# Mixer output contracted over 128 + 64 channels, the last 64 of two tiles side by side on halves of the rows

## The chip, the cores and the metric

The kernel runs on one core of one Trainium2 chip. The metric is the time of one execution on the device in microseconds; a smaller number is better. The core has a matrix engine (TensorE, PE in the profile, with its weight loads as PEld), a vector engine (DVE), a scalar engine (ACT), GpSimd (POOL), and SyncE (SP), which here only starts DMA transfers. Each engine works through its own instructions in order, and they wait for each other at semaphores.

## The reference

An input of 32 images, 56 x 56 pixels with 96 channels, goes through two layers. Layer 0 is attention in shifted windows of 7 x 7 and a quantized feed-forward part. Layer 1 is a mixer with a recurrence along the width, and another feed-forward part of the same kind. Each part is added to its input, after a layer normalization. What matters here is the mixer:

```python
x = _layernorm(inputs, ln_gamma, ln_beta)
x_proj = jnp.einsum('bhwc,ce->bhwe', x, W_expand)
gate = jax.nn.sigmoid(jnp.einsum('bhwc,ce->bhwe', x, W_gate))
ssm_out = _ssm_scan(x_proj, A, B, C, D)
gated = gate * ssm_out
return jnp.einsum('bhwe,ec->bhwc', gated, W_out)
```

Here `c` runs over 96 channels and `e` over 192. The last line, which contracts the 192 gated channels to 96, is what the change concerns.

## The kernel before

A block is 14 image rows (784 pixels), held as 7 tiles `g` of 112 pixels by 96 channels in `xb`. There are 128 blocks, four to an image. All work on a block is cut into about a hundred named steps, such as `q` (queries and keys), `sc` (scores), `av` (values), `hf0` to `yf` (feed-forward of layer 0), `pu0` to `pu3` (the mixer's two projections), `gt0`, `gt1`, `so` (its output) and `hg0` to `yg` (feed-forward of layer 1). Steps that begin with `h` or `y` and end in `f` or `g` belong to the layer with that letter: `hf` and `yf` to layer 0, `hg` and `yg` to layer 1.

The order of the work is written out by hand in tables: `PIPELINED`, with `FILL` for the first 7 rounds and `DRAIN` for the last ones. In round `t` an entry `name:lag` runs step `name` for block `t - lag`. So each engine has a fixed order, in which some 11 blocks overlap. The six scan steps `SC0` to `SC5` and their gates `GA0` to `GA5` run once for a whole image, in one round of four.

All PSUM tiles come from one pool of four buffers of two banks each (`banks`), so a step on PE also waits until an earlier step's result has been read out of the buffer that it gets.

In the mixer, the scan leaves its gated result in `gts`, with pixels of a row pair on the partitions (two rows of 56 in 64 each) and 192 channels along the free side. To contract over channels, PE first transposes: `gt0` does tiles 0 to 3 and `gt1` tiles 4 to 6, each tile as two halves of 96 channels, L884. ACT copies the results to `gT` (steps `eg0`, `eg1`, L894), whose partitions 96 to 127 are zero. Step `so` then multiplies each tile in two matmuls that add up in PSUM, one for each half of 96 channels, L905: 14 matmuls over 128 rows of the array, of which 96 hold data. Step `as` (L513, shared with `ad`) adds the result to `xb` on DVE.

Float32 matmuls show as two records each in the profile; transposes show as one. A matmul has a tile of the array: all 128 x 128, or a part of it such as 64 x 64 (the scans and `av`), 128 x 64 (`q`, `v`), 128 x 32 (`k`) or 32 x 64 (`sc`); parts that don't overlap can work at the same time. The profile writes rows and columns as `64*64`.

Of the kernel before, what the change touches and what calls it, by code (L numbers as in the profile page):

```python
# [8 lines left out]
F32 = mybir.dt.float32  # L9
# [4 lines left out]
ALU = mybir.AluOpType  # L14
# [9 lines left out]
C = 96  # L24
HW = 56
# [5 lines left out]
E = 2 * C  # L31
EH = E // 2
RS = 64
UNIT = 16
NS = 16
TP = 2 * HW
G = 7
NBLK = 4
# [15 lines left out]


PIPELINED = (
    "rf2:4 r0:5 hf0:4 GA2:9 cf1:4 SC0:9 zg:11 GA0:9 ex2:3 ex0:3 pu1:5 SC5:9 xf0:4 pu0:5 th1:5 av:3 "
    "cf2:4 GA5:9 bg:11 uc1:5 pu2:5 th0:5 sa:1 rc:3 ta:2 rf0:4 uc0:5 uc2:5 th2:5 cf0:4 pa:1 ea:2 pg:10 "
    "tro:3 yf:4 eo:3 kg:11 gt0:9 zf:4 pr:3 ng:10 pu3:5 bf:4 eg0:9 kf:4 ad:3 th3:5 sf:3 uc3:5 pf:3 k:2 "
    "tg:10 se:4 ek:2 pe:4 SC1:8 gt1:9 eg:10 eg1:9 q:2 GA1:8 eq:2 hg0:10 nf:3 xg0:10 hg1:10 rg0:10 "  # L60
    "SC3:8 xg1:10 ne:4 so:9 SC4:8 as:9 hg2:10 GA3:8 ST:11 v:2 tf:3 cg0:10 GA4:8 xg2:10 sc:2 ev:2 te:4 "
    "ef:3 rg1:10 hf1:3 xe:4 rg2:10 cg2:10 cg1:10 st1:2 st2:2 xf1:3 ex1:2 hf2:3 xf2:3 SC2:8 st0:2 "
    "yg:10 sg:9 na:1 LD:0 rf1:3 "
)

FILL_ROUNDS = 7
FILL = (
    "gt0:9 hf0:4 r0:5 SC1:8 gt1:9 pu0:5 xf0:4 pg:10 ex2:3 hg1:10 SC2:8 ex0:3 pu1:5 eg:10 GA0:9 rf2:4 "
    "cf1:4 pu2:5 xg1:10 th1:5 uc0:5 th2:5 SC5:9 rg1:10 ng:10 uc1:5 th0:5 ST:11 cg0:10 rg0:10 uc2:5 "
    "cf2:4 sa:1 rf0:4 av:3 cf0:4 eg0:9 so:9 SC0:9 rc:3 kg:11 sg:9 GA2:9 zg:11 GA5:9 GA3:8 yf:4 zf:4 "  # L70
    "tro:3 as:9 cg2:10 bf:4 kf:4 se:4 pa:1 ta:2 xg2:10 eo:3 GA1:8 rg2:10 ea:2 pe:4 pr:3 q:2 k:2 ad:3 "
    "ek:2 bg:11 LD:0 yg:10 tg:10 pu3:5 uc3:5 cg1:10 sf:3 GA4:8 eq:2 th3:5 v:2 ne:4 ev:2 te:4 pf:3 "
    "sc:2 xe:4 nf:3 tf:3 st1:2 ef:3 st0:2 st2:2 ex1:2 hf1:3 eg1:9 xf1:3 hg2:10 xg0:10 na:1 SC4:8 "
    "hg0:10 hf2:3 xf2:3 SC3:8 rf1:3 "
)
DRAIN_FROM = 2
DRAIN = (
    "hf0:4 rf2:4 cf2:4 r0:5 SC5:9 xf0:4 LD:0 pu3:5 v:2 zg:11 pu2:5 uc3:5 eq:2 bg:11 st0:2 rf0:4 pg:10 "
    "pu1:5 ex0:3 GA2:9 sa:1 cf1:4 th3:5 q:2 cf0:4 GA5:9 ng:10 th2:5 kg:11 ex2:3 uc2:5 yf:4 uc1:5 na:1 "
    "SC0:9 GA0:9 st1:2 sc:2 th1:5 av:3 gt0:9 rc:3 zf:4 st2:2 bf:4 ea:2 tro:3 eo:3 eg0:9 ek:2 tg:10 "  # L80
    "pr:3 pu0:5 eg:10 ad:3 gt1:9 hg2:10 sf:3 uc0:5 kf:4 se:4 eg1:9 pf:3 xg2:10 th0:5 SC4:8 nf:3 "
    "hg0:10 tf:3 hg1:10 ta:2 rg2:10 xg1:10 pe:4 cg2:10 SC3:8 rg1:10 ef:3 pa:1 ne:4 xg0:10 GA4:8 "
    "cg1:10 GA3:8 rg0:10 so:9 cg0:10 as:9 ev:2 hf1:3 hf2:3 SC2:8 ST:11 ex1:2 te:4 xf2:3 yg:10 xf1:3 "
    "SC1:8 xe:4 GA1:8 sg:9 rf1:3 k:2 "
)

IN_TURN = (
# [10 lines left out]
def kernel(  # L98
# [27 lines left out]
    nc = tc.nc  # L126
# [3 lines left out]
    const = ctx.enter_context(tc.tile_pool(name="const", bufs=1))  # L130
# [8 lines left out]
    def banks(name):  # L139

        return psum.tile([128, 2, 512], F32, tag="ps", name=name)
# [15 lines left out]
    xtiles = {}  # L157
# [3 lines left out]
    def zeros(size, name):  # L161
        t = const.tile([128, size], F32, name=name)
        nc.gpsimd.memset(t, 0.0)
        return t

    wqkv = zeros(3 * C, "wqkv")
    ident = zeros(128, "ident")
# [2 lines left out]
    wo = zeros(C, "wo")  # L170

    weg = zeros(2 * E, "weg")
    wso = zeros(2 * C, "wso").rearrange("p (h c) -> p h c", h=2)
    mask = zeros(W2, "mask")
    low = zeros(W2, "low")
# [22 lines left out]
    gts = [const.tile([128, NRP, E], F32, name=f"gt_{n}") for n in range(2)]  # L198
# [55 lines left out]
    n = 1  # L254
# [18 lines left out]
    pt = banks("tapsT")  # L273
# [47 lines left out]
    for par in range(2):  # L321
        half = mask[par * 64 : par * 64 + 64, :]
# [3 lines left out]
        half = low[par * 64 : par * 64 + 64, :]  # L326
# [15 lines left out]
    pt = banks("bias1")  # L342
# [25 lines left out]
    for n, (w1, b1_, w2, b2_) in enumerate(((f0_w1, f0_b1, f0_w2, f0_b2), (f1_w1, f1_b1, f1_w2, f1_b2))):  # L368
        w1s = stage(128, 3 * C).rearrange("p (h c) -> p h c", h=3)
        nc.scalar.dma_start(w1s, w1.rearrange("(h p) c -> p h c", p=128))  # L370
        pt = banks(f"w1t_{n}")
# [7 lines left out]
        pt = banks(f"w2t_{n}")  # L379
# [21 lines left out]
    nc.scalar.dma_start(bet, beta[:, None])  # L401
    nc.scalar.dma_start(weg[0:C, 0:E], w_gate)
    nc.scalar.dma_start(weg[0:C, E : 2 * E], w_expand)
    nc.scalar.dma_start(wso[0:C], ssm_w_out.rearrange("(h p) c -> p h c", p=C))


    xws, vs, gTs, xqs = [], [], [], []
    for n in range(2):
        xw = const.tile([128, NTOK + OVER], F32, name=f"xw_{n}")
        nc.vector.memset(xw[C:, :], 1.0)  # L410
        nc.vector.memset(xw[0:C, NTOK:], 0.0)
        xws.append(xw)
        gT = const.tile([128, 4 - n, 2, TP], F32, name=f"gT_{n}")
        nc.vector.memset(gT[C:], 0.0)
        gTs.append(gT)
        xq = const.tile([128, NTOK], F8, name=f"xq_{n}")
        nc.vector.memset(xq[C:], 0.0)
        xqs.append(xq)
        v = const.tile([128, NPAIR * NH, HD + 1], F32, name=f"v_{n}")
        nc.vector.memset(v[:, :, HD:], 1.0)  # L420
        vs.append(v)
    ot = const.tile([128, G, 2 * NPAIR, WS], F32, name="ot")
    nc.vector.memset(ot[C:], 1.0)

# [12 lines left out]
    held = {}  # L437

    def steps(*names):


        def enter(f):
            if len(names) == 1:
                step[names[0]] = f
            else:
                for k, n in enumerate(names):
                    step[n] = lambda i, k=k: f(i, k)
            return f

        return enter  # L450
# [50 lines left out]
    def out_banks(name):  # L501

        po = banks(name)
        return [
            (g0, g1, po[0:TP, k, 0 : (g1 - g0) * C].rearrange("p (g c) -> p g c", c=C))
            for k, (g0, g1) in enumerate(((0, 4), (4, G)))
        ]

    def add_out(n):
        def add(i):  # L510
            xb = xtiles[i]
            for g0, g1, po in held.pop((n, i)):
                nc.vector.tensor_tensor(xb[:, g0:g1, :], po, xb[:, g0:g1, :], ALU.add)  # L513

        return add

    @steps("LD")
    def _(i):
        xb = xpool.tile([TP, G, C], F32, tag="xb", name=f"xb_{i}")
        for dst, src in block_dmas(i, x, xb):  # L520
            nc.sync.dma_start(dst, src)
        xtiles[i] = xb
# [190 lines left out]

    @steps("pr")
    def _(i):
        held["pr", i] = out_banks(f"pr_{i}")
        for g0, g1, po in held["pr", i]:
            for g in range(g0, g1):
                nc.tensor.matmul(po[:, g - g0, :], ot[:, g].rearrange("c w b -> c (w b)"), wo, start=True, stop=True)  # L719

# [154 lines left out]
    halves = ((0, 4), (4, G))  # L875

    @steps("gt0", "gt1")
    def _(i, k):
        g0, g1 = halves[k]
        pt = banks(f"gt_{i}_{k}")  # L880
        for g in range(g0, g1):
            for eh in range(2):
                s = (g - g0) * 2 + eh
                nc.tensor.transpose(  # L884
                    pt[0:C, s // 4, (s % 4) * 128 : (s % 4 + 1) * 128],
                    gts[i // NBLK % 2][:, (i % NBLK) * G + g, eh * EH : (eh + 1) * EH],
                    ident,
                )
        held["gt", i, k] = pt

    @steps("eg0", "eg1")
    def _(i, k):
        n = 4 * (halves[k][1] - halves[k][0])
        nc.scalar.copy(  # L894
            gTs[k][0:C].rearrange("c g h (r w) -> c (g h r) w", w=HW)[:, 0:n],
            held.pop(("gt", i, k))[0:C].rearrange("c b (s w) -> c (b s) w", w=RS)[:, 0:n, 0:HW],
        )

    @steps("so")
    def _(i):  # L900
        held["so", i] = out_banks(f"so_{i}")
        for gT, (g0, g1, po) in zip(gTs, held["so", i]):
            for g in range(g0, g1):
                for eh in range(2):
                    nc.tensor.matmul(  # L905
                        po[:, g - g0, :], gT[:, g - g0, eh, :], wso[:, eh, :], start=(eh == 0), stop=(eh == 1)
                    )

    step["as"] = add_out("so")
    feed_forward("g", 1)  # L910
# [88 lines left out]
```

## Time and profile before

| | |
|---|---|
| time, median of 3 runs | 3842.33 us (3831.57 to 3846.85) |
| the profiled execution's own time | 3844.57 us |
| its span, first to last instruction | 3842.8 us |
| mean granted TensorE clock | 0.988 |
| `so`, L905: 3584 matmul records | 377.5 us busy, 263 ns each |
| `gt`, L884: 1792 matmul records | 243.1 us busy, 276 ns each |
| copies of `gt`, L894: 256 on ACT | 209.4 us busy, 818 ns each |
| PE busy from 1000 to 2000 us | 987.13 us |

The profile has one line for each group of instructions: source line, engine, operation, result and operands, for a matmul the tile of the array, the shape, then how many. Busy time is the time in which at least one of them ran. Matmuls overlap each other in the pipeline, so the duration of one (263 ns for `so`) is more than what each adds. A timeline row merges instructions that follow each other with the same line and names: start, length, engine, line, and how many. The distance between the starts of two rows that follow each other is what the first one costs on a full engine.

### The profile page before, as it was taken

How to read it: one execution, taken by the hardware profiler on the slowest of the kernel's cores; microseconds unless marked ns; L12 is line 12 of the kernel's file. 1: busy time of each engine (PE TensorE's matmuls, PEld its weight loads, DVE VectorE, ACT ScalarE, POOL GpSimd, SP SyncE). 2: the span in 40 equal slices, each digit the busy share in tenths (PEclk: the TensorE clock that was granted, in tenths of full speed). 3: DMA queues.
4: the chain of work that ended last, by engine and by line, in shares of the span. 5: the costliest groups of instructions: out<-in, count | busy, mean ns of one | idle time of the engine just before them, and what ended most of it. 6: DMA issues, size and time to landing. Idle time of an engine off the chain costs nothing.

```text
span 3842.8 us, 178057 instructions
## 1 busy us (share of the span) xinstructions
PE 3695.3 (96%) x78628; PEld 3124.7 (81%) x78628; DVE 3247.2 (84%) x9420; ACT 2329.9 (61%) x4611; POOL 1452.0 (38%) x1176
## 2 busy tenths in 40 slices
PE   4899999999999999999999999999999999999996
PEld 3788888888888888888888888888888888888875
DVE  6788888988888888888888888888888888888875
ACT  2666666666666666566666666665566666656662
POOL 2333334443333443333443333443333433333432
PEclk8999999999999999999999999999999999999997
DMA  6001001101001111000101100101100101100100
GB/s 136 14 12 25 22 22 25 25 23 27 22 22 24 26 25 25 22 22 23 27 22 25 25 22 22 28 22 25 25 22 22 28 22 23 27 22 22 25 15 21
DMA packets 226267, 99.34 MB, mean 26 GB/s; under 512 B 218396, under 2 KB 225150, under 8 KB 225262
## 3 DMA queue, kind: packets, MB, share of 16 engines
q1 hardware_dynamic: 222522, 86.81, 10.0%
q8 instruction: 620, 10.16, 1.1%
q10 hardware_dynamic: 2964, 1.05, 0.1%
q14 instruction: 161, 1.32, 0.1%
HBM read 44.45 MB, written 43.35 MB: 23 GB/s over the span
## 4 chain that ended last, share of the span: by engine, by line
PE 91%; DVE 6%; issue 2%; ACT 1%; POOL 0%; DMA 0%; SPq 0%; DVEq 0%; ACTq 0%; POOLq 0%
PE pu L827 13%; PE scan L851 10%; PE so L905 9%; PE qk L547 8%; PE av L671 5%; PE gt L884 5%; PE pv L566 5%; PE pr L719 5%; PE pu L828 4%; PE s L589 4%; DVE pT L620 4%; PE ph_g L739 4%; PE py_g L773 4%; PE py_f L773 4%; PE tr_o L700 3%; PE ph_f L739 3%
## 5 line engine op out<-in xcount | busy, mean ns | idle before, releaser
L827 PE MATMUL pu<-weg,xs 128*128 128x288 f32 x1792 | 618.6, 427 | 2.0 <-issue 1.7
L751 ACT CAST h_g<-ph_g 128x784 f16<-128x784 f32 x384 | 300.5, 820 | 332.6 <-issue 326.0
L481 DVE TENSOR_SCALAR xn_g<-xb,st_g,rs_g 112x96 fp8e5<-112x96 f32 x896 | 365.0, 476 | 95.1 <-POOL rs_g L471 94.4
L851 PEld LDWEIGHTS scan<-u,toep 64*64 64x64 f32 x24576 | 387.8, 135 | 62.8 <-issue 42.4
L851 PE MATMUL scan<-u,toep 64*64 64x28 f32 x24576 | 413.9, 221 | 17.4 <-issue 16.4
L828 PEld LDWEIGHTS pu<-weg,xs 128*128 128x128 f32 x1792 | 339.8, 190 | 98.1 <-issue 3.5
L840 ACT COPY u<-pu 128x384 f32<-128x384 f32 (+1 forms) x512 | 229.1, 448 | 291.4 <-PE pu L828 235.3
L763 POOL CAST hq_g<-h_g 128x784 fp8e5<-128x784 f16 x128 | 122.1, 954 | 730.4 <-DVE h_g L757 461.2
L471 POOL TENSOR_TENSOR rs_a<-rs_a,neg_half 112x7 f32<-112x7 f32 x128 | 190.7, 1490 | 502.7 <-DVE rs_a L465 502.7
L905 PEld LDWEIGHTS so<-wso,gT 128*112 128x112 f32 x3584 | 372.5, 179 | 9.8 <-issue 0.9
L905 PE MATMUL so<-wso,gT 128*112 128x96 f32 x3584 | 377.5, 263 | 0.2 <-ACT h_g L751 0.2
L835 ACT ACTIVATE gt<-pu 128x384 f32<-128x384 f32 (+1 forms) x512 | 237.7, 464 | 205.9 <-PE pu L828 205.9
L866 DVE SCALAR_TENSOR_TENSOR gt<-gt,scan 128x448 f32<-128x448 f32 x384 | 220.6, 617 | 144.5 <-PE scan L851 144.4
L828 PE MATMUL pu<-weg,xs 128*128 128x96 f32 x1792 | 321.2, 261 | 3.4 <-issue 3.3
L547 PE MATMUL qk<-xw,wqkv 128*32 128x196 f32 (+1 forms) x3072 | 310.5, 394 | 4.8 <-issue 2.5
L751 ACT CAST h_f<-ph_f 128x784 f16<-128x784 f32 x384 | 308.8, 806 | 3.0 <-issue 2.8
L795 POOL TENSOR_TENSOR xb<-xb,y_f 112x672 f32<-112x672 f32 x128 | 187.3, 1463 | 293.3 <-DVE y_f L791 293.3
L827 PEld LDWEIGHTS pu<-weg,xs 128*128 128x128 f32 x1792 | 276.0, 191 | 18.7 <-issue 3.0
L620 DVE SCALAR_TENSOR_TENSOR pT<-s,bias 128x392 f32<-128x392 f32 (+1 forms) x512 | 213.7, 459 | 68.7 <-PE s L589 64.3
L739 PEld LDWEIGHTS <-w1q 128*128 128x128 fp8e5 x1536 | 123.7, 100 | 173.7 <-issue 81.3
L894 ACT COPY gT<-gt 96x896 f32<-96x896 f32 (+1 forms) x256 | 209.4, 818 | 76.4 <-PE gt L884 73.5
L481 DVE TENSOR_SCALAR xn_f<-xb,st_f,rs_f 112x96 fp8e5<-112x96 f32 x896 | 226.2, 326 | 33.4 <-POOL rs_f L471 33.4
(147 smaller groups left out, 8608.2 us busy)
## 6 DMA issues: line engine op xcount, KB each, us to landing
xb<-in_x_dram SPq DMA_DIRECT2D x224, 126.0 KB
out_dram<-xb SPq DMA_DIRECT2D x224, 126.0 KB
taps_d<-u SPq DMA_DIRECT2D x1, 4704.0 KB
xb<-in_x_dram SPq DMA_DIRECT2D x224, 13.1 KB
xb<-in_x_dram SPq DMA_DIRECT2D x224, 7.9 KB
out_dram<-xb SPq DMA_DIRECT2D x224, 13.1 KB
out_dram<-xb SPq DMA_DIRECT2D x224, 7.9 KB
xb<-in_x_dram SPq DMA_DIRECT2D x32, 72.0 KB
```

Of the source, the lines that this page charges most:

```text
L481: nc.vector.tensor_scalar(xn[:, g, :], xb[:, g, :], mean[:, col], rs[:, col], op0=ALU.subtract, op1=ALU.mult, **saturate)
L547: nc.tensor.matmul(pq[j * rows : (j + 1) * rows, m, 0:size], wqkv[:, m * C + h0 * HD : m * C + h1 * HD], xws[i % 2][:, j * size : (j + 1) ...
L620: nc.vector.scalar_tensor_tensor(view(dst), src, QSCALE, view(bt), op0=ALU.mult, op1=ALU.add)
L739: nc.tensor.matmul(ph[:, half, 0:HALF], w1q[:, hc * 128 : (hc + 1) * 128], xqs[layer][:, half * HALF : (half + 1) * HALF], start=True, sto ...
L751: nc.scalar.copy(h16.rearrange("p (h t) -> p h t", h=2), held.pop(("ph", n, i, hc))[:, :, 0:HALF])
L773: nc.tensor.matmul(po[:, g - g0, :], hq[hc][:, g * TP : (g + 1) * TP], w2q[:, hc, :], start=(hc == 0), stop=(hc == 2),)
L827: nc.tensor.matmul(pu[:, g, 0 : E + EH], rows[:, 0:128], weg[:, 0 : E + EH], start=True, stop=True)
L828: nc.tensor.matmul(pu[:, g, E + EH : 2 * E], rows[:, RS:], weg[:, E + EH :], start=True, stop=True)
L835: nc.scalar.activation(gt[:, rp : rp + n, :], held["pu", i, j][:, 0:n, 0:E], AF.Tanh, scale=0.5)
L840: nc.scalar.copy(u[:, rp : rp + n, :], held["pu", i, j][:, 0:n, E : 2 * E])
L851: nc.tensor.matmul(py[o0 : o0 + RS, eh, e * NRP : (e + 1) * NRP], toep[p * RS : (p + 1) * RS, ch * HW : ch * HW + RS], u[p * RS : (p + 1) ...
L905: nc.tensor.matmul(po[:, g - g0, :], gT[:, g - g0, eh, :], wso[:, eh, :], start=(eh == 0), stop=(eh == 1))
```

## The change

The 192 channels are contracted as 128 + 64, not as 96 + 96. The first 128 of each tile take a matmul on all rows of the array. The last 64 of an even tile lie on partitions 0 to 63 of the new buffer `gTb`, those of an odd tile on partitions 64 to 127, and their matmuls use only that half of the rows, against a copy of the same 64 rows of the weights in each half of `wso`. Even tiles go to one PSUM bank, odd tiles to the other. That makes 7 matmuls on the full array and 7 on halves of it, where there were 14 on the full array.

The transposes follow: one of 128 channels for each tile to the first bank; in the second bank, one of channels 64 to 191 for each odd tile, which leaves the last 64 on the upper partitions, and then one of the last 64 channels of each even tile, written over the lower ones. In `gt1` the last tile stands in for the odd tile that is missing. It is 15 transposes in a block, where there were 14. ACT makes four copies of them in place of two. All three tables of the order are new.

```diff
 PIPELINED = (
-    "rf2:4 r0:5 hf0:4 GA2:9 cf1:4 SC0:9 zg:11 GA0:9 ex2:3 ex0:3 pu1:5 SC5:9 xf0:4 pu0:5 th1:5 av:3 "
-    "cf2:4 GA5:9 bg:11 uc1:5 pu2:5 th0:5 sa:1 rc:3 ta:2 rf0:4 uc0:5 uc2:5 th2:5 cf0:4 pa:1 ea:2 pg:10 "
-    "tro:3 yf:4 eo:3 kg:11 gt0:9 zf:4 pr:3 ng:10 pu3:5 bf:4 eg0:9 kf:4 ad:3 th3:5 sf:3 uc3:5 pf:3 k:2 "
-    "tg:10 se:4 ek:2 pe:4 SC1:8 gt1:9 eg:10 eg1:9 q:2 GA1:8 eq:2 hg0:10 nf:3 xg0:10 hg1:10 rg0:10 "
-    "SC3:8 xg1:10 ne:4 so:9 SC4:8 as:9 hg2:10 GA3:8 ST:11 v:2 tf:3 cg0:10 GA4:8 xg2:10 sc:2 ev:2 te:4 "
-    "ef:3 rg1:10 hf1:3 xe:4 rg2:10 cg2:10 cg1:10 st1:2 st2:2 xf1:3 ex1:2 hf2:3 xf2:3 SC2:8 st0:2 "
-    "yg:10 sg:9 na:1 LD:0 rf1:3 "
+    "q:2 SC4:8 pf:3 rg2:10 xg1:10 k:2 nf:3 GA3:8 GA4:8 rg1:10 eq:2 pe:4 hg0:10 ne:4 v:2 SC2:8 cg1:10 "
+    "cg2:10 xg0:10 ek:2 ev:2 tf:3 rg0:10 ef:3 so:9 cg0:10 GA2:8 te:4 sc:2 as:9 xe:4 st1:2 st2:2 ST:11 "
+    "r0:4 hf2:3 st0:2 xf2:3 ex1:2 ex2:2 yg:10 zg:10 hf1:3 ex0:2 xf1:3 sg:9 SC0:8 pg:9 rf2:3 bg:10 "
+    "GA0:8 pu0:4 th0:4 hf0:3 rf1:3 SC5:8 LD:0 uc0:4 cf1:3 pu1:4 ng:9 GA5:8 av:2 xf0:3 rc:2 pa:1 rf0:3 "
+    "uc1:4 th1:4 gt0:8 eg0:8 tg:9 cf0:3 pu2:4 tro:2 pu3:4 kg:10 cf2:3 eg:9 yf:3 uc2:4 th2:4 sa:0 eo:2 "
+    "uc3:4 pr:2 zf:3 na:1 bf:3 th3:4 SC1:7 ad:2 ta:1 GA1:7 gt1:8 hg2:9 ea:1 sf:2 kf:3 eg1:8 hg1:9 "
+    "SC3:7 xg2:9 se:3 "
 )
...
-    nc.scalar.dma_start(wso[0:C], ssm_w_out.rearrange("(h p) c -> p h c", p=C))
+    nc.scalar.dma_start(wso[:, 0], ssm_w_out[0:128])
+    for p0 in (0, 64):
+        nc.scalar.dma_start(wso[p0 : p0 + 64, 1], ssm_w_out[128:E])
...
-        gT = const.tile([128, 4 - n, 2, TP], F32, name=f"gT_{n}")
-        nc.vector.memset(gT[C:], 0.0)
-        gTs.append(gT)
...
+    gTa = const.tile([128, G, TP], F32, name="gTa")
+    gTb = const.tile([128, (G + 1) // 2, TP], F32, name="gTb")
...
-            for g0, g1, po in held.pop((n, i)):
-                nc.vector.tensor_tensor(xb[:, g0:g1, :], po, xb[:, g0:g1, :], ALU.add)
+            for part, po in held.pop((n, i)):
+                xb = xtiles[i][:, part, :]
+                nc.vector.tensor_tensor(xb, po, xb, ALU.add)
...
         for g in range(g0, g1):
-            for eh in range(2):
-                s = (g - g0) * 2 + eh
+            nc.tensor.transpose(pt[:, 0, (g - g0) * 128 : (g - g0 + 1) * 128], gt[:, g, 0:128], ident)
+
+
+        for half in (1, 0):
+            for m in range(2):
+                g = min(g0 + 2 * m + half, G - 1)
                 nc.tensor.transpose(
-                    pt[0:C, s // 4, (s % 4) * 128 : (s % 4 + 1) * 128],
-                    gts[i // NBLK % 2][:, (i % NBLK) * G + g, eh * EH : (eh + 1) * EH],
-                    ident,
+                    pt[0 : 64 + 64 * half, 1, m * 128 : (m + 1) * 128], gt[:, g, 128 - 64 * half : E], ident
                 )
...
-        n = 4 * (halves[k][1] - halves[k][0])
-        nc.scalar.copy(
-            gTs[k][0:C].rearrange("c g h (r w) -> c (g h r) w", w=HW)[:, 0:n],
-            held.pop(("gt", i, k))[0:C].rearrange("c b (s w) -> c (b s) w", w=RS)[:, 0:n, 0:HW],
-        )
+        g0, g1 = halves[k]
+        pt = held.pop(("gt", i, k)).rearrange("c b (s w) -> c b s w", w=RS)[:, :, :, 0:HW]
+        for b, dst in ((0, gTa[:, g0:g1]), (1, gTb[:, 2 * k : 2 * k + 2])):
+            dst = dst.rearrange("c g (r w) -> c (g r) w", w=HW)
+            nc.scalar.copy(dst, pt[:, b, 0 : dst.shape[1]])
...
-        held["so", i] = out_banks(f"so_{i}")
-        for gT, (g0, g1, po) in zip(gTs, held["so", i]):
-            for g in range(g0, g1):
-                for eh in range(2):
-                    nc.tensor.matmul(
-                        po[:, g - g0, :], gT[:, g - g0, eh, :], wso[:, eh, :], start=(eh == 0), stop=(eh == 1)
-                    )
+        po = banks(f"so_{i}")[0:TP]
+        dst = lambda g: po[:, g % 2, g // 2 * C : (g // 2 + 1) * C]
+
+        for g in range(G):
+            nc.tensor.matmul(dst(g), gTa[:, g, :], wso[:, 0, :], start=(g < 2), stop=False)
+
+        for g in range(G):
+            half = slice(g % 2 * 64, g % 2 * 64 + 64)
+            nc.tensor.matmul(dst(g), gTb[half, g // 2, :], wso[half, 1, :], start=False, stop=(g >= G - 2))
+        held["so", i] = []
+        for b in range(2):
+            n = (G + 1 - b) // 2
+            held["so", i].append((slice(b, G, 2), po[:, b, 0 : n * C].rearrange("p (g c) -> p g c", c=C)))
```

`FILL` and `DRAIN` are replaced in the same way. On PE the new `PIPELINED` gives this order in a round, with the scans where a group has them: `q SC4 k hg0 v SC2 tf so te sc hf2 yg hf1 SC0 pu0 hf0 SC5 pu1 av gt0 tg pu2 tro pu3 yf pr SC1 ta gt1 hg2 hg1 SC3`. Before, it was `hf0 SC0 pu1 SC5 pu0 av pu2 ta tro yf gt0 pr pu3 k tg SC1 gt1 q hg0 hg1 SC3 so SC4 hg2 v tf sc te hf1 hf2 SC2 yg`.

## The prediction

> **What bounds the kernel now.** I read the page first, then the chain of waits, the waits of PE, the sums by stretch, and last the timeline of PE, which carries the argument.
>
> ```profile
> PE 3695.3 (96%) x78628; PEld 3124.7 (81%) x78628; DVE 3247.2 (84%) x9420; ACT 2329.9 (61%) x4611; POOL 1452.0 (38%) x1176
> ...
> PE 91%; DVE 6%; issue 2%; ACT 1%; POOL 0%; DMA 0%; SPq 0%; DVEq 0%; ACTq 0%; POOLq 0%
> ```
>
> On the page PE is busy 96% and is 91% of the chain. Next one round without scans, 25.3 us, and one with the six scan steps of a group, 39.6 us (columns: stretch, its length, busy PE, PEld, DVE, ACT, POOL, clock, DMA):
>
> ```profile
> 2066.30:2091.60 25.30, 25.11 (x425) 21.14 (x423) 23.48 (x72) 17.94 (x36) 11.23 (x9) 1.00 0.11 26
> ...
> 2116.90:2156.50 39.60, 39.23 (x1076) 33.32 (x1077) 34.11 (x98) 23.03 (x45) 12.68 (x11) 1.00 0.08 19
> ```
>
> Four rounds take 115.5 us, 32 times over. DVE works 23.5 of 25.3 us, so it is close behind. PE's largest wait from 300 to 3600 us (total, times, longest):
>
> ```profile
> PE ph_f L739 <- DVE pT L620: 21.3, 113, 0.2
> ```
>
> A busy PE isn't a useful PE: what counts is from one step's start to the next one's.
>
> ```profile
> 2021.33 0.54 PE L494 MATMUL tr_g<-ident,xn_g 112*96 112x112 fp8e5 x7
> 2021.80 2.07 PE L851 MATMUL scan<-u,toep 64*64 64x28 f32 x128
> 2023.80 0.86 PE L884 MATMUL gt<-ident,gt 128*96 128x128 f32 x6
> 2024.59 1.54 PE L547 MATMUL qk<-xw,wqkv 128*64 128x392 f32 x8
> ...
> 2028.83 2.99 PE L905 MATMUL so<-wso,gT 128*112 128x96 f32 x28
> 2031.75 0.44 PE L851 MATMUL scan<-u,toep 64*64 64x28 f32 x16
> ```
>
> ```profile
> 2056.84 1.04 PE L884 MATMUL gt<-ident,gt 128*96 128x128 f32 x8
> 2057.71 1.52 PE L719 MATMUL pr<-wo,ot 128*112 128x96 f32 x14
> ...
> 2060.68 0.55 PE L494 MATMUL tr_g<-ident,xn_g 112*96 112x112 fp8e5 x7
> 2061.06 0.82 PE L884 MATMUL gt<-ident,gt 128*96 128x128 f32 x6
> 2061.81 1.54 PE L547 MATMUL qk<-xw,wqkv 128*64 128x392 f32 x8
> 2063.28 0.84 PE L739 MATMUL ph_g<-xq,w1q 128*128 128x392 fp8e5 x4
> 2063.96 2.90 PE L905 MATMUL so<-wso,gT 128*112 128x96 f32 x28
> 2066.69 0.50 PE L739 MATMUL ph_g<-xq,w1q 128*128 128x392 fp8e5 x2
> 2067.12 1.54 PE L566 MATMUL pv<-wqkv,xw 128*64 128x96 f32 x32
> 2068.59 0.54 PE L494 MATMUL tr_f<-ident,xn_f 112*96 112x112 fp8e5 x7
> ```
>
> Between full-array steps `so` takes 2066.69 - 2063.96 = 2.73 us, 28 records (two to a float32 matmul) of 98 ns. Eight transposes take 0.87 us, 109 ns each. But `so` between two scans, which run on 64x64 tiles, takes 2.92. `tr_g` takes 0.38 before `gt` and 0.47 before a scan. The six transposes take 0.75 after `tr_g` and 0.79 after a scan, and both before `qk` on 128x64 tiles, where six of 109 ns make 0.65. So leaving a tile shape costs 0.094 us each time, and arriving 0.04 (`gt`) to 0.09 (`so`, whose first weights are then not loaded ahead). Small tiles pay for themselves by running side by side: `pv` does 32 records in 1.47 us; by the records' own starts a pair takes 0.083, and four of a scan 0.058.
>
> **What the Trainium skill says.** "TensorEngine Tiling (Array Packing)", Key Properties: changing the tiling mode, not only the tile, drains TensorE. The trace agrees: the 0.094 us above. The same page, Overview, gives up to 2x for a side of 64 or less; `pv` agrees for column halves, and so do the scans, whose four tiles share rows and columns. Its Restrictions say that column tiling excludes transpose mode for FP32 input; no transpose before is on such a tile, so the trace doesn't show it. "TensorE: Matmul & The Clock Gate", LDWEIGHTS: load time goes with columns, columns / 1.2 ns, whatever the rows; 112 columns are 93 ns, and `so` runs at 98.
>
> **The change part by part,** for a round, on PE. Tile shapes and neighbours are from the changed program's instruction order.
>
> `so`. Seven 128-row matmuls: 14 records, 1.36 us. Drain to 64x128 tiles: 0.094. Seven 64-row ones alternate between two row halves and two banks, four to three. If a pair costs what one does, by the load, that is 8 slots of 98 ns: 0.78, not 1.37. Arriving and leaving this shape: `pv` pays 1.47 - 16 x 0.083 = 0.15, its first load 64 columns; for 112 I take 0.185 (bounds 0.10 and 0.25). The next step, `te`, arrives anew: 0.04. Sum 2.46 against 2.73: -0.27.
>
> `gt0`. Six transposes of 128 columns; `pu` L828 with 128-column loads runs at 112 ns, so 0.67. Drain 0.094, two 64-column transposes 0.22, arriving and leaving 0.125 (0.09 to 0.16), next step 0.037. Sum 1.15 against 0.88: +0.27. The two narrow ones may not be single-pass on that tile: from nothing to 0.22 more here, and in `gt1` again. I take nothing: they are still issued as transposes.
>
> `gt1`. Five wide, two narrow: 0.56 + 0.094 + 0.22 + 0.125 + 0.006 before `hg2`. Sum 1.00 against 0.66 without its old drain to `q`: +0.35.
>
> Other visits to small tiles, by the new table. Before, `av`, `k`, `q`, `v` and `sc` each stand alone between full steps: 0.465 leaving, 0.197 arriving. After, `q` and `k` adjoin and the steps behind have cheaper arrivals: 0.458 together. -0.20.
>
> Scans, per four rounds. Before, six lone visits: 0.889. After, `SC4` stands between `q` and `k`, `SC2` behind `v`, `SC3` before `q`; three are lone: 0.469. -0.42.
>
> Four rounds: 4 x (-0.27 + 0.27 + 0.35 - 0.20) - 0.42 = +0.2 us, about +5 us in 32. In the whole program changes of shape go from 1640 to 2196: the halved products earn 0.59 x 128 = 75 us, and drains and transposes spend it.
>
> So waits decide. PE's four rounds without any wait sum to 112.35 us before, from its steps' usual times and these drains; the trace has 115.5: 3.2 us of waits, 100 in all. Half of it is one wait: the second `ph_f` starts 0.69 us after the first, where 0.17 is a run of them, because its bank waits until DVE has read the scores (`pT` L620). In the new order `hf2` takes the bank that `so` left, and `hf1` that of `hf2`; the score banks go to `pu0` and `hf0`, 1.76 and 3.18 us after `sc`, when DVE is done 1.7 after. That stall goes. Next late is DVE: I laid its new order along PE's by hand with the durations of before; `xn_a` is done 0.4 us before `ta` wants it, `xn_f` 0.6 before `tf`, and `GA5` 0.9 before `gt0`. With a scan round, `SC0` and `SC5` wait for no bank, where they waited 0.4 and 0.2. I take 1.5 us left per four rounds (bounds 0.8, the irregular rest, and 4): -1.7 x 32 = -54.
>
> At nothing: `gT` evicted by four copies, not two (163 ns + 0.87 per column from the 192 and 384 column `th`: 1.72 us against 1.63, ACT being 39% idle; uncovered it is 0.1 us per round), and `so`, behind which all of PE would queue, finds `gTb` written some 4 us before in that layout; the added output in strided slices of the same size; two more loads of `wso` on ACT's queue, first used near 210 us; two memsets fewer; `turn_toep` a round earlier, its table landed by 78 us and DVE there at 95 before, some 86 after, while PE still idles. Stores wait on SP for POOL's last add, then loads for stores: some 8 us, against about 24 from `kg:10` to the next round's `sa:0`, and 1176 POOL instructions keep their sizes. Ramp and drain I hold at +-10.
>
> Sum: span 3842.8 + 5 - 54 = 3794. The profiled execution was 3844.6, the median 3842.3, so this reads 3794 on the median's scale too; a little ramp for the finer steps, +4, gives 3798.
>
> **Rivals.** (1) The waits only move: DVE at 93% binds where I left it 0.4 us. For it: the slack is less than one `xn_a`. Against: the old order shows no such wait. 3842 + 5 = 3847, +-15. (2) Slower: the 64-row products don't run side by side. Place: L916 of the new kernel; price 6 x 98 ns x 128 = 75 us; it decides as soon as fewer than about five of the six pairings hold, and with the gain of waits it is 3873, without 3920. Against it: the scans. Two-pass narrow transposes, 4 x 109 ns x 128 = 56, would give 3854. (3) The change does more: waits at 0.8 and the drains of these two steps at their low bounds (0.15 us a round, 19 in all): 3842 + 5 - 77 - 19 = 3751 to 3775.
>
> **How the numbers follow.** Forecast 0.54 (own range 3770 to 3830), waits that move 0.20, slower 0.14, more 0.12. About 0.5%, 19 us, is what a measurement can tell: below 3823 is faster. Faster: 0.43 of the forecast, 0.12 of more, 0.01 of moving waits: 0.56. Same: 0.11 + 0.14 + 0.02 = 0.27. Slower: 0.05 of moving waits, 0.12 of the slower case: 0.17. The range takes in the low case and most of the slow one: 3750 to 3880.
>
> **What would show it.** `so` at 2.3 to 2.5 us from start to start, its last 14 records in 0.8 to 1.0; `gt` steps near 1.1 and 1.0; a round without scans at 25.0 to 25.2; no `ph_f` wait for `pT`. Wrong if the 64-row records start 98 ns apart, if narrow transposes have two records each, or if PE waits for `xn_a` or `xn_f` in every round.

## The result, and the profile after

The changed kernel takes 3752.7 us (median of 4 runs, 3752.2 to 3755.4), where the kernel before took 3844.2 us beside it: a ratio of 0.977, 95% interval 0.9747 to 0.9792. The forecast was 3798 us. The profiled execution took 3752.4 us, its span is 3750.7 us; its mean granted TensorE clock is 0.984, where it was 0.988.

The page after, busy time of the engines and the chain that ended last:

```profile
PE 3623.0 (97%) x78756; PEld 3079.2 (82%) x78756; DVE 3140.3 (84%) x9418; ACT 2327.9 (62%) x4867; POOL 1427.9 (38%) x1176
...
PE 94%; DMA 2%; issue 2%; DVE 2%; POOL 1%; ACT 0%; SPq 0%; ACTq 0%; POOLq 0%; DVEq 0%
```

PE's chain share rose from 91% to 94%, and the 6% of DVE fell to 2%. The sums by stretch, for one round without scans and one with them (columns as in the prediction):

```profile
2125.22:2149.80 24.58, 24.58 (x426) 20.78 (x424) 22.54 (x71) 17.97 (x38) 11.03 (x9) 1.00 0.07 16
2086.68:2125.22 38.54, 37.62 (x1193) 32.72 (x1192) 29.33 (x83) 18.40 (x38) 11.12 (x9) 1.00 0.12 27
```

A round without scans is 24.6 us, where it was 25.3, and PE is busy in all of it. One with scans takes 38.5, where it took 39.6. From one `so` to the fourth one after it, four rounds take 112.4 us in the median, in place of 115.4; over the some 30 such periods in the steady part that is about 91 us, nearly the whole gain of 92 us between the spans. The first scan starts at 176.4 us as before.

PE's waits from 300 to 3500 us, the two largest, after:

```profile
PE scan L855 <- issue: 14.9, 20, 1.4
PE qk L550 <- issue: 4.2, 5, 1.1
```

"issue" stands for a wait for nothing that the profile shows. The wait of `ph_f` for `pT`, 20.5 us in this window before, does not occur any more. Last, the timeline of PE with the changed steps: `so`, then `gt0`, then `gt1`:

```profile
2131.99 1.57 PE L912 MATMUL so<-wso,gTa 128*112 128x96 f32 x14
2133.49 1.02 PE L916 MATMUL so<-wso,gTb 64*112 64x96 f32 x14
2134.44 0.88 PE L499 MATMUL tr_e<-ident,xn_e 112*96 112x112 f32 x7
...
2143.03 0.66 PE L887 MATMUL gt<-ident,gt 128*128 128x128 f32 x4
2143.52 0.60 PE L893 MATMUL gt<-ident,gt 128*128 128x128 f32 x4
2143.95 0.51 PE L497 MATMUL tr_g<-ident,xn_g 112*96 112x112 fp8e5 x7
...
2150.47 0.49 PE L887 MATMUL gt<-ident,gt 128*128 128x128 f32 x3
2150.80 0.60 PE L893 MATMUL gt<-ident,gt 128*128 128x128 f32 x4
2151.24 0.83 PE L743 MATMUL ph_g<-xq,w1q 128*128 128x392 fp8e5 x4
```

From `so` to `tr_e` it is 2134.44 - 2131.99 = 2.45 us, the forecast's figure, with 0.95 for the 64-row half. `gt0` takes 2143.95 - 2143.03 = 0.92 where 1.15 was forecast, `gt1` 2151.24 - 2150.47 = 0.77 where 1.00 was. The row of L893 holds wide and narrow transposes alike, and a row shows the shape of its first record only. With the shapes kept apart they are two groups over the whole run, busy time and the mean ns of one behind the bar:

```profile
L893 PE MATMUL gt<-ident,gt 128*128 128x128 f32 x512 | 98.9, 275 | 0.0
L893 PE MATMUL gt<-ident,gt 128*64 128x128 f32 x512 | 98.7, 275 | 0.0
```

What the profile writes as rows and columns is what a matmul uses, and need not be its tile of the array (`so` is 128*112). The narrow transposes are marked 128*64, but in the single records they follow the wide ones at the same 109 ns, with no drain between.

### The profile page after: what moved, and what is told of

It reads as the page before. It is cut to its first block, busy times and chain, and to the rows that moved or that the text cites. A ratio compares the mean times of both kernels' runs of the same rounds, so it can differ in the third digit from the quotient of the medians.

```text
span 3750.7 us, 179098 instructions
## 1 busy us (share of the span) xinstructions
PE 3623.0 (97%) x78756; PEld 3079.2 (82%) x78756; DVE 3140.3 (84%) x9418; ACT 2327.9 (62%) x4867; POOL 1427.9 (38%) x1176
## 4 chain that ended last, share of the span: by engine, by line
PE 94%; DMA 2%; issue 2%; DVE 2%; POOL 1%; ACT 0%; SPq 0%; ACTq 0%; POOLq 0%; DVEq 0%
PE pu L831 12%; PE scan L855 11%; PE qk L550 8%; PE av L674 5%; PE pv L569 5%; PE so L912 5%; PE pr L723 5%; PE pu L832 5%; PE s L592 4%; PE ph_g L743 4%; PE ph_f L743 4%; PE py_f L777 4%; PE py_g L777 3%; PE so L916 3%; PE gt L887 3%; PE tr_o L703 3%
## 5 line engine op out<-in xcount | busy, mean ns | idle before, releaser
L831 PE MATMUL pu<-weg,xs 128*128 128x288 f32 x1792 | 608.5, 421 | 2.4 <-ACT h_f L755 1.2
L755 ACT CAST h_g<-ph_g 128x784 f16<-128x784 f32 x384 | 302.6, 837 | 122.7 <-PE ph_g L743 112.4
L755 ACT CAST h_f<-ph_f 128x784 f16<-128x784 f32 x384 | 316.9, 827 | 76.4 <-PE ph_f L743 70.2
L810 ACT ACTIVATE xs<-tr_e,bet,gam 96x448 f32<-96x448 f32 (+1 forms) x256 | 158.6, 668 | 269.3 <-PE tr_e L499 269.3
L474 POOL TENSOR_TENSOR rs_g<-rs_g,neg_half 112x7 f32<-112x7 f32 x128 | 202.9, 1585 | 319.8 <-DVE rs_g L468 319.8
L820 POOL COPY xs<-xs 96x392 f32<-96x392 f32 x128 | 65.7, 513 | 673.7 <-issue 662.5
L484 DVE TENSOR_SCALAR xn_g<-xb,st_g,rs_g 112x96 fp8e5<-112x96 f32 x896 | 295.6, 397 | 30.2 <-POOL rs_g L474 30.1
L484 DVE TENSOR_SCALAR xn_e<-xb,st_e,rs_e 112x96 f32<-112x96 f32 x896 | 287.9, 390 | 0.2 <-POOL rs_e L474 0.2
L474 POOL TENSOR_TENSOR rs_f<-rs_f,neg_half 112x7 f32<-112x7 f32 x128 | 201.1, 1571 | 183.4 <-DVE rs_f L468 183.4
L550 PEld LDWEIGHTS qk<-xw,wqkv 128*32 128x32 f32 (+1 forms) x3072 | 117.6, 119 | 165.3 <-issue 69.2
L904 ACT COPY gTa<-gt 128x448 f32<-128x448 f32 (+1 forms) x256 | 125.3, 490 | 193.9 <-PE gt L893 183.7
```

The source lines that it names most:

```text
L474: nc.gpsimd.tensor_tensor(rs, rs, neg_half, ALU.pow)
L484: nc.vector.tensor_scalar(xn[:, g, :], xb[:, g, :], mean[:, col], rs[:, col], op0=ALU.subtract, op1=ALU.mult, **saturate)
L550: nc.tensor.matmul(pq[j * rows : (j + 1) * rows, m, 0:size], wqkv[:, m * C + h0 * HD : m * C + h1 * HD], xws[i % 2][:, j * size : (j + 1) ...
L755: nc.scalar.copy(h16.rearrange("p (h t) -> p h t", h=2), held.pop(("ph", n, i, hc))[:, :, 0:HALF])
L831: nc.tensor.matmul(pu[:, g, 0 : E + EH], rows[:, 0:128], weg[:, 0 : E + EH], start=True, stop=True)
```

## The experiments

Each ran beside the kernel before; ratios are to that. The time of a step is the median from its start to that of the next step, over the steady part of the run.

**The parts apart.** `tables_only` is the kernel before with the three new tables; `code_only` is the kernel after with the three old ones.

```diff
 # tables_only, from the kernel before
 PIPELINED = (
-    "rf2:4 r0:5 hf0:4 GA2:9 cf1:4 SC0:9 zg:11 GA0:9 ex2:3 ex0:3 pu1:5 SC5:9 xf0:4 pu0:5 th1:5 av:3 "
...
+    "q:2 SC4:8 pf:3 rg2:10 xg1:10 k:2 nf:3 GA3:8 GA4:8 rg1:10 eq:2 pe:4 hg0:10 ne:4 v:2 SC2:8 cg1:10 "
...
 # code_only, from the kernel after
 PIPELINED = (
-    "q:2 SC4:8 pf:3 rg2:10 xg1:10 k:2 nf:3 GA3:8 GA4:8 rg1:10 eq:2 pe:4 hg0:10 ne:4 v:2 SC2:8 cg1:10 "
...
+    "rf2:4 r0:5 hf0:4 GA2:9 cf1:4 SC0:9 zg:11 GA0:9 ex2:3 ex0:3 pu1:5 SC5:9 xf0:4 pu0:5 th1:5 av:3 "
...
```

> The kernel before (96 + 96 channels, 14 full-array products) run in the order of the new tables. Theory A (the new order brings most of the gain, by fewer lone visits to small tiles and by waits that go; the 128 + 64 contraction itself earns about 0.1 us a block): against the changed kernel's 3753 us, so costs 2.73 instead of 2.46 us, te after it 0.04 less, gt0 and gt1 together 0.15 less, so about +0.10 us x 128 = +13: 3766 us, 3755 to 3780. Theory B (the contraction brings the gain, as the words of the change say): the time stays within 20 us of the kernel before, 3825 to 3845. In both the second ph_f should no longer wait for pT.

> The changed kernel run in the order of the old tables. Theory A: so at 2.46 us and gt1 one transpose longer, about -0.15 us x 128 = -19: 3825 us, 3810 to 3840, with the ph_f wait for pT still there. Theory B: 3750 to 3780.

`tables_only`: 3782.1 us, 0.9821 (0.9792 to 0.985). `code_only`: 3842.4 us, 0.9988 (0.9974 to 1.0001). So the tables alone bring 64 us, the code alone about 3, both 92: by these medians the code is worth 29 us in the new order and 3 in the old. `tables_only` ended just above the range of its theory A, and both expectations of `code_only` were wrong. Its steps changed as in the new tables (`so` 2.41, `gt0` 0.89, `gt1` 0.87 where it was 0.75 in that order), a net 0.18 us in a round without scans. But the old wait is there as before, in PE's waits from 300 to 3500 us,

```profile
PE ph_f L743 <- DVE pT L623: 21.0, 109, 0.2
```

and the rounds with scans grew by some 0.4 us, so that four rounds are 115.3 us, next to 115.4. The granted clock differs too. In the trace of `code_only` it is 0.50 in four stretches of 20.5 us together, from 300 to 3500 us, which costs some 10 us of full clock; in that of the kernel before it is full all the way. The medians of the clocks on record, 0.984 and 0.987, say the same: 0.003 of 3842 us is about 12 us (an estimate; of the 15 runs of the kernel before beside it, the one at 0.983 took 3859.9 us and those at 0.988 took 3841.7 to 3845.8). By this estimate the code earns some 13 to 15 us in the old order, where the medians show 3 and theory A forecast 19.

**The pairs of 64-row products.** `unpaired` issues the even tiles' products first and then the odd ones'; `same_half` puts all seven on rows 0 to 63.

```diff
 # unpaired
-        for g in range(G):
+        for g in (0, 2, 4, 6, 1, 3, 5):
 # same_half
-            half = slice(g % 2 * 64, g % 2 * 64 + 64)
+            half = slice(0, 64)
```

> The changed kernel with the 64-row products of so issued as four even tiles and then three odd ones, so that neighbours use the same half of the rows. Theory A (two row halves work side by side only when they alternate): 14 slots of 98 ns in place of 8, +0.59 us a block, so at 3.04 us and 3753 + 75 = 3828 us, 3810 to 3840. Rival (issue order doesn't matter, or the halves never overlapped): no change, 3745 to 3760.

> The kernel after, with all seven 64-row products of so on rows 0 to 63, so that no two of them can work side by side. The odd tiles are multiplied with the last 64 channels of the even tile beside them, so their outputs change; the work is the same. Theory A: the pairs are what so gains by. The trace shows a pair of records every 98 ns; six records more on the path are 6 x 98 ns = 0.59 us a round, 75 us in all: so at 3.04 us and 3828 us (3815 to 3840), slower than the old so of 2.73 us. Theory B: the array overlaps neighbouring products anyway, as it did in part when even and odd tiles were issued one after the other (so at 2.73 us, +52 us): 3790 to 3812.

`unpaired`: 3804.0 us, 0.988 (0.9852 to 0.9908), `so` 2.73. `same_half`: 3839.9 us, 0.9975 (0.9964 to 0.9987), `so` 3.05. The timeline of `same_half`:

```profile
2180.64 1.57 PE L912 MATMUL so<-wso,gTa 128*112 128x96 f32 x14
2182.15 1.61 PE L916 MATMUL so<-wso,gTb 64*112 64x96 f32 x14
2183.69 0.88 PE L499 MATMUL tr_e<-ident,xn_e 112*96 112x112 f32 x7
```

The 64-row half is 2183.69 - 2182.15 = 1.54 us, 0.59 more than in pairs, to the hundredth what six records of 98 ns are. So the halves do work side by side, and without that this `so` is slower than the old one. `unpaired` loses half of it only, and lands between its two expectations: by its single records the odd tiles' first products overlap the last even ones, though they were issued behind them. That is 35 us; the rest of its 51 lies in the rounds with scans.

**The narrow transposes.** `narrow_mm` makes the transposes of 64 channels ordinary float32 products with the identity.

```diff
-                nc.tensor.transpose(dst, src, ident)
+                if half:
+                    nc.tensor.transpose(dst, src, ident)
+                else:
+                    nc.tensor.matmul(dst, src, ident, start=True, stop=True)
```

> The changed kernel with the four narrow transposes of a block issued as ordinary float32 products with the identity on the same 128 x 64 tile; the values are the same. Theory A (what spared gt the drains is that a transpose doesn't change the tile shape of the array; a product does): each has two records, 0.22 us more for gt0 and for gt1, and each step gets two drains and arrivals, about 0.26 us; together 0.96 us a block, 3753 + 123 = 3876 us, 3850 to 3900. Rival (128 x 64 after 128 x 128 never drains here): the second records alone, 0.44 us a block, 3753 + 56 = 3809 us, 3800 to 3820.

3874.9 us, 1.0072 (1.0043 to 1.01), as theory A had it. The timeline of its `gt0`:

```profile
2142.53 0.65 PE L887 MATMUL gt<-ident,gt 128*128 128x128 f32 x4
2143.02 0.38 PE L896 MATMUL gt<-ident,gt 128*128 128x128 f32 x2
2143.33 0.65 PE L898 MATMUL gt<-ident,gt 128*64 128x128 f32 x4
2143.91 0.55 PE L497 MATMUL tr_g<-ident,xn_g 112*96 112x112 fp8e5 x7
```

The narrow ones have a line of their own here, so the row shows their shape, 128*64, the same as that of the narrow transposes; but they have two records each. And the first one starts 0.20 us after the last wide one, where a narrow transpose started 0.11 after: 0.09 more, which is the prediction's drain. The step takes 1.38 us, 0.46 more. So a product on 64 columns pays for a change of tile shape, and a transpose on 64 columns doesn't; the shape that the profile prints is the same for both and can't tell them apart.

**One transpose less.** In `gt1` the last tile stands in for a missing odd one; `no_standin` leaves that out, and `eg1` copies tile 6 from 64 partitions.

```diff
-                g = min(g0 + 2 * m + half, G - 1)
+                g = g0 + 2 * m + half
+                if g == G:
+                    continue
...
+        if k:
+            parts.append((pt[0:64, 1, 2:], gTb[0:64, 3:4]))
```

> The kernel after, without the transpose in gt1 in which the last tile stands in for the missing odd tile: 14 transposes in a block, not 15. The second copy of eg1 becomes two, one of tile 5 with tile 4 on 128 partitions and one of tile 6 on 64. Theory A: PE has no wait left in a round without a scan, so each transpose is on the path with its 109 ns: 128 x 0.109 us = 14 us less, 3739 us (3734 to 3745). Theory B: other waits take it, such as those for instructions in the scans, or the added copy delays ACT: 3748 to 3760.

3747.4 us, 0.9739 (0.9723 to 0.9756). `gt1` is 0.658 us, where it was 0.767: the 109 ns are on the path, but the medians differ by 5 us, not 14, just below theory B's range: the waits for "issue" at `scan` and `qk` are 24.7 us from 300 to 3500 us in its trace, next to 19.1. It is the lowest time measured; its interval overlaps that of the changed kernel.

**A local move in the new tables.** `so_by_v` moves `so` in `PIPELINED` to in front of `tf`, and issues the 64-row products first.

```diff
-"ev:2 tf:3 rg0:10 ef:3 so:9 cg0:10"
+"ev:2 so:9 tf:3 rg0:10 ef:3 cg0:10"
...
-            nc.tensor.matmul(dst(g), gTa[:, g, :], wso[:, 0, :], start=(g < 2), stop=False)
+            half = slice(g % 2 * 64, g % 2 * 64 + 64)
+            nc.tensor.matmul(dst(g), gTb[half, g // 2, :], wso[half, 1, :], start=(g < 2), stop=False)
...
-            half = slice(g % 2 * 64, g % 2 * 64 + 64)
-            nc.tensor.matmul(dst(g), gTb[half, g // 2, :], wso[half, 1, :], start=False, stop=(g >= G - 2))
+            nc.tensor.matmul(dst(g), gTa[:, g, :], wso[:, 0, :], start=False, stop=(g >= G - 2))
```

> The kernel after, with so moved in PIPELINED to right behind v and the scan there (in front of tf), and its 64-row products in front of its full ones. Theory A: v is on 64 rows, tf and te on all: the change to a smaller tile in so, its drain of 0.09 to 0.19 us, falls in with that behind v, and tf follows full products; some 0.08 us a round, 10 us: 3743 us (3730 to 3748). Theory B: nothing is saved, since the array changes its tile as often as before between q and te and the arrivals only move (3750 to 3756), or more, if the scores' second buffer, now that of so, waits for as on DVE (3757 to 3775, with a wait of PE s for DVE in the trace).

3859.0 us, 1.0027 (1.0015 to 1.0039). `so`, `tf` and `te` did get 0.13 us shorter together, but theory B's wait came, at a greater price; PE's largest wait, of `so_by_v`:

```profile
PE s L586 <- DVE xb L510: 45.0, 83, 0.8
```

The scores' second buffer is now the one of `so`, and the addition `as` that frees it stands behind `xn_e` on DVE: `s` takes 2.08 us in a round without scans, where it took 1.28.

**What the new tables do, tried in the old ones.** Three kernels, each the one before with entries of `PIPELINED` moved; `code_te_yg` is the second with the new code.

```diff
 # te_first
-"sc:2 ev:2 te:4 ef:3 rg1:10 hf1:3 xe:4"
+"te:4 sc:2 ev:2 ef:3 rg1:10 hf1:3 xe:4"
 # te_yg_first: that, and
-"hf2:3 xf2:3 SC2:8 st0:2 yg:10"
+"SC2:8 yg:10 hf2:3 xf2:3 st0:2"
 # te_yg_sa: both, and
-"sa:1 rc:3 ta:2"
+"rc:3 sa:1 ta:2"
```

> The kernel before, with one entry of PIPELINED moved: te stands before sc, no longer behind it. FILL and DRAIN are untouched. Theory A: most of what the new tables bring comes from one wait. hf2 got a buffer of the scores, which DVE had not read yet, and stood 0.47 us behind it in each round; with te in front it gets te's buffer, and the wait is gone: 0.47 us x 124 rounds = 58 us, some of it spent again in other waits, so 3795 us (3782 to 3810), and ph_f shows no wait for pT. Theory B: PE only moves the wait to the next step that gets a buffer of the scores, since DVE is what sets the pace there: 3835 to 3850, with an equal wait before yg or the next scan.

> The kernel before, with the order of five steps in PIPELINED as the new table has it: te, sc, a first hf, yg, the other hf, where it was sc, te, hf1, hf2, (SC2,) yg. The rest of the old tables stays. When te alone went in front of sc, yg was given the buffer of hf1, whose copy stands on ACT behind two copies of te, and PE waited 0.5 us for it in each round (3895 us). Here yg is given the buffer of te, and hf2 that of hf1, which has 1.1 us more. Theory A: the wait of 0.47 us a round is gone and no other comes in its place; 0.47 us x 124 = 58 us less, 3788 us (3778 to 3805), close to the 3782 us of the new tables with the old code: the tables bring little else. Theory B: the copies on ACT are late for yg too (those of te end about when yg would start), 0.2 to 0.5 us a round: 3815 to 3890.

> The new code of gt0, gt1, eg and so in the same table as te_yg_first. Theory A: the new code gains what its steps gain in any table in which PE waits for nothing else there: so 0.27 to 0.33 us less, gt0 0.01 and gt1 0.12 more, 0.18 us a round net, 23 us less than te_yg_first: some 3765 us (3755 to 3780). Its small effect in the old tables (3 us) came from scan rounds that grew by 0.4 us. Theory B: the new code is worth little in any order but the new table's: less than 8 us below te_yg_first.

> The kernel of te_yg_first (old code, old tables with te, sc, hf1, yg, hf2), with one more entry moved: sa (st_a and rs_a on DVE, 1.31 us) stands behind rc (which writes an), no longer in front of it. Theory A: in the old order DVE needs 10.67 us from the start of the scores on PE to the end of an, without a gap, and tro on PE waits for an; this stretch is what PE could not win against, wherever its own wait lay. Shorter by 1.31 us it is 9.37 us, against 10.07 us that PE needs from the scores to tro, so tro waits no more and PE keeps what its order saves: 0.38 us a round against the kernel before, 48 us: 3800 us (3785 to 3815). Theory B: DVE is late as a whole and the wait moves on, to py_f or tr_a: 3860 to 3916, as without the move (3916).

All were slower than the kernel before, and outside all that was expected but for theory B of `code_te_yg`: `te_first` 3895.1 us, 1.0119 (1.01 to 1.0139); `te_yg_first` 3916.5 us, 1.0169 (1.0144 to 1.0194); `code_te_yg` 3914.0 us, 1.0166 (1.0126 to 1.0206); `te_yg_sa` 4080.2 us, 1.0593 (1.0551 to 1.0636). PE's largest wait in `te_first`, in `te_yg_first`, and the two largest in `te_yg_sa`, from 300 to 3500 us:

```profile
PE py_g L773 <- ACT h_f L751: 39.6, 81, 0.6
```

```profile
PE tr_o L700 <- DVE an L690: 45.0, 76, 0.7
```

```profile
PE py_f L773 <- DVE hq_f L763: 56.5, 103, 0.6
PE gt L884 <- DVE xb L513: 53.5, 78, 0.7
```

The old wait is gone from each, and each has another in its place. In `te_first` it is for the buffer of `hf1`, whose copy stands on ACT behind those of `te`; given another buffer, PE stands at `tr_o`. DVE's timeline before says why, from the scores on (the last row is PE's):

```profile
2070.42 1.70 DVE L620 SCALAR_TENSOR_TENSOR pT<-s,bias 128x392 f32<-128x392 f32 x4 [0.28 <-PE s L589]
...
2073.30 1.76 DVE L481 TENSOR_SCALAR xn_a<-xb,st_a,rs_a 112x96 f32<-112x96 f32 x7
...
2078.78 0.96 DVE L690 TENSOR_TENSOR an<-av,sm 128x768 f32<-128x768 f32 x1
...
2080.18 1.04 PE L700 MATMUL tr_o<-ident,an 128*96 128x128 f32 x8
```

DVE works from 2070.42 to 2079.74 without a gap and then hands `an` to `tr_o`, 0.44 us before that starts. From the first product of the scores to the end of `an` it is 10.67 us (median) before and 10.68 in `te_yg_first`. With `te` in front of the scores PE has less to do in that stretch, so it arrives at `tr_o` early and stands.

With the new code as well (`code_te_yg`) this wait stays as long: 49.4 us in 81 waits, where it was 45.0 in 76. The gain of the code, which lies outside the stretch, doesn't go into it: a round without scans takes 25.5 us, where it took 25.7 in `te_yg_first`. That the two kernels' medians are alike goes with the granted clock, 0.970 to 0.978 in the four runs of `code_te_yg` and 0.979 to 0.982 in four of the five of `te_yg_first`. The two runs nearest in clock, at 0.978 and 0.979, took 3907.3 and 3921.5 us. So theory A of `code_te_yg`, 23 us for the code, is not refuted, though its total was far off.

In `te_yg_sa` the stretch is 9.42 us and the wait of `tr_o` is gone, as theory A said; but `st_a` is later, GpSimd makes `rs_g` behind `rs_a`, so DVE waits 2.2 us a round for `rs_g`, and `xn_g` and all behind it are late. That the wait moves on is what theory B said; the time is 160 us above its range.

**The same stretch in the new tables.** After, `xn_a` stands behind `tr_o`, and the stretch is 9.51 us, with 1.0 us to spare before `tr_o`. `na_back` moves it into the stretch again.

```diff
-"te:4 sc:2"
+"te:4 pa:1 sc:2"
...
-"sg:9 SC0:8"
+"sg:9 na:1 SC0:8"
...
-"rc:2 pa:1 rf0:3"
+"rc:2 rf0:3"
...
-"zf:3 na:1 bf:3"
+"zf:3 bf:3"
```

> The kernel after, with na (xn_a, 1.77 us on DVE) moved in PIPELINED to behind sg, between the scores and an, where the old tables had it; pa (a step of GpSimd that na needs) moves in front of sc. Theory A: the new tables gain by taking xn_a out of the stretch on DVE from the scores to an (9.51 us, where it was 10.67, with 1.0 us left before tro). With 1.77 us more in it, of which DVE's short waits there absorb some 0.5, an is late for tro by 0.4 to 0.9 us a round: 3800 to 3865 us, with a wait of tr_o for an in the trace. Theory B: the place of xn_a does not matter, since DVE has idle time enough: 3750 to 3758, no such wait.

3904.4 us, 1.0125 (1.0081 to 1.0168): theory A in direction, above its range in size. PE's largest wait, of `na_back`:

```profile
PE tr_g L497 <- DVE xn_g L484: 47.3, 81, 0.6
```

The wait is not where I put it. `xn_g` stands in front of `an` on DVE, and `tr_g` on PE in front of `tr_o`; so `tr_g` waits, for one piece of `xn_g` after the other, 1.91 us from start to start where it was 0.35. In this order the place of `xn_a` is worth more than the whole change. It is not the old order's stretch that comes back, though: with the waits it is 11.7 us here, a microsecond longer than it was before.

## Why the prediction was right, and where it was not

Direction and both mechanisms held: the 64-row products pair, and the waits shrink. The time was 45 us too high, inside the range; the gain was about twice the forecast.

- **`so`, -0.27:** measured 2.456 us against 2.46 forecast, the 64-row half 0.95. The pairing holds (`same_half`), so the slower rival fell at its decisive point.
- **Waits, 1.5 us left per four rounds, -54:** measured 1.5 to 1.65, nearly all in scan rounds. The `ph_f` wait is gone. The rival of waits that only move did not come true here, but it is what happened in all four trials in the old tables and in `so_by_v`. My account of it, other banks, was a part of it: besides, DVE's stretch to `an` became 1.16 us shorter, which I had laid out by hand, and not priced. How much each of the two brings was not measured apart.
- **`gt0` +0.27 and `gt1` +0.35: the mis-sized terms.** Both took the narrow transposes for a visit to a tile of 64 columns: a drain of 0.094, arriving and leaving 0.125. Measured: 0.929 and 0.767 in place of 1.15 and 1.00, because the narrow transposes paid for no such visit. `narrow_mm` shows that the price is real, 0.46 us a step with the two records, where the narrow ones are products. The two terms, 0.22 + 0.23 us a round, are 1.8 us per four rounds: with them the +0.2 of the forecast becomes -1.6, and the sum of the steps without waits went from 112.35 to about 110.8, -1.55. Over 32 groups that is 58 us, and the miss was 45. Some 6 us of the difference are there because the gain was had in 30 groups and not in 32; some of the rest can be the granted clock, which the forecast took as unchanged: after, 20.5 us of the trace ran at half clock, and before none. The remainder was not resolved.
- **Ramp +4:** start and end were unchanged within 1 us.
- **The rival of more, 3751 to 3775:** its time came true, and in part by luck. It names the cost of these two steps, but took 0.15 us a round off it where 0.45 was due, and it took 0.8 us of waits where 1.5 to 1.65 stayed; the two errors offset each other.

"TensorEngine Tiling (Array Packing)" of the Trainium skill, Restrictions, excludes column tiling for FP32 transposes. The runs fit this in that the transposes with 64 columns of data paid no drain and took one pass of 109 ns, where products of the same shape paid one; the profile marks both 128*64, so the mode itself is not shown. I cited this sentence and then priced the transposes as tiled all the same. Its drain on a change of tiling mode stands, for products.

Left open: why the rounds with scans grew in `code_only`, and why the granted clock was lower there and in `code_te_yg`. That savings of the code end in waits for DVE is shown for neither.

## What to carry to other kernels

Before a tile shape is priced, look whether the operation takes one: a transpose on half the columns cost what a full one does, a product there cost a drain. When an engine waits in a kernel whose second engine is nearly as busy, measure the unbroken stretch of that second engine between two hand-overs, and compare it with what the first engine has to do meanwhile. Here moving the waiting step alone moved the wait, and shortening the stretch by 1.26 us in `te_yg_sa` removed this wait but made others elsewhere. When the same code gains 29 us in one order and 3 in another, compare the granted clocks before looking for waits: by the estimate above some 10 us of the difference went with the clock.

## What the runs showed of the hardware that was not expected

The waits that are left are 26 stalls of over 0.3 us from 300 to 3500 us, 24 of them put down to "issue". All lie in a scan, where PE runs through 128 small matmuls in 2.0 us, or at most 17 records behind its end. Each comes with one 16 KB packet on the queue of PE's instructions (623 in the run, one for some 126 matmuls) that lands 1.2 to 1.6 us before PE goes on: the one at 744.5 us began 0.19 us after its packet had landed and lasted 1.19 us. By this PE seems to run out of instructions where they are small and dense. No run tested it; the stalls of this kind came to 17 us in the trace before and to 26 in `tables_only`.

Second, such a stall can cost more than its length. Behind six of the 26, within 1.1 us of their end, the granted clock was 0.50 for 3.4 us. A `so` that fell into one took 4.04 us in place of 2.46 (the last line has the columns of the sums by stretch):

```profile
1311.67 0.65 PE L855 MATMUL scan<-u,toep 64*64 64x28 f32 x27 [0.98 <-issue]
...
1312.63 2.82 PE L912 MATMUL so<-wso,gTa 128*112 128x96 f32 x14
...
1316.67 0.88 PE L499 MATMUL tr_e<-ident,xn_e 112*96 112x112 f32 x7
```

```profile
1312.70:1316.10 3.40, 3.40 (x25) 3.23 (x24) 0.81 (x2) 0.86 (x2) 0.00 (x0) 0.50 0.03 5
```

The 14 traces have 81 such stretches in this window, of 3.4 to 23.9 us each, and at 80 of them a stall of over 0.3 us ended less than 2 us before or was still going on. But the kernel before has 29 such stalls and not one such stretch, so a stall alone isn't enough, and what else it takes stays open. They sum to 20.5 us in the kernel after and to 133 in the profiled run of `te_yg_first`, the slowest of its five. Differences of 10 or 20 us between kernels should be read with the clock beside them.

Third, products on two halves of the rows overlapped, for 0.31 us of the 0.59 that full pairing saves, even where all of one half were issued before the other (`unpaired`).
